# Record slots in two arrays, blockwise normalizations and a shorter node stage in a four-layer graph network

## The chip, the cores and the metric

The kernel runs on one core of a Trainium2 chip. The metric is the device time of one execution in microseconds (us). Engines are named as in the profile: PE (matrix products), PEld (its weight loads), DVE (vector), ACT (scalar), POOL (GpSimd) and SP (which here issues transfers). "L359" is line 359 of the kernel before.

## The reference

A graph of 6,250 nodes with 64 features each and 206,250 directed edges (each of 100,000 drawn edges in both directions, and a loop at each node), with 64 features and one of four types per edge. Each layer normalizes the nodes and adds its result to them:

```python
h = relu(layernorm(x)); x = x + L0(h)   # attention: softmax over each node's incoming edges
h = relu(layernorm(x)); x = x + L1(h)   # degree-normalized graph convolution
h = relu(layernorm(x)); x = x + L2(h)   # messages, below
h = relu(layernorm(x)); x = x + L3(h)   # gated graph network: 4 steps, a sum per edge type, then a GRU cell

def L0(h):
    qk, v = h @ qk_w.T + qk_b, h @ v_w.T + v_b
    s = clip(sum(qk[dst] * qk[src]) / 8, -5, 5)
    out = segment_sum(softmax_over(dst, s) * v[src], dst) @ o_w.T + o_b
    return layernorm(out + h) * ln_g + ln_b

def L2(h):
    f = relu([h[src], h[dst], edge] @ W1_f + b1_f) @ W2_f + b2_f    # summed at dst
    r = relu([h[dst], h[src], edge] @ W1_r + b1_r) @ W2_r + b2_r    # summed at src
    agg = segment_sum(f, dst) + segment_sum(r, src)
    return h + relu([agg, h] @ Wn1 + bn1) @ Wn2 + bn2
```

## The kernel before

Nodes stand in NB = 49 blocks of P = 128, and the blocks of destinations in NG = 7 groups of GB = 7. W = 7 x 128 = 896.

**Sort.** The kernel first sorts the edges by pairs of blocks (destination, source). Each edge gets a record of RW = 70 floats (six small fields and its 64 features) and a slot in a DRAM array, `rec_d`. The array has 7 x 50 = 350 tiles (NC = 50: one for each source block, and one more, the overflow of the pair of a block with itself, whose edges include the loops). A tile has 896 slots: 128 ranks for each of 7 destination blocks, rank first. Slots that no edge takes must hold an empty record (-1 in the first four fields, then zeros), so ACT's queue first fills the array: seven transfers (L215) with 128 rows of 25 packets of 3,920 bytes each, all from one small SBUF tile, `fill`.

Meanwhile DVE derives everything that the sort needs of the keys, in instructions over all EC = 1,620 columns (the edges as 128 x 1,620): block numbers `bd` and `bs`, six fields `cf`, the pair's `key`, the slot's `base` (L221 to L251). The keys go transposed to DRAM (`row_d`, L244). The first normalization follows, then a loop over 162 groups of G = 10 columns (`order`, written out by hand for PE, ACT, DVE and SP). In each group:

- `load`: SP loads the transposed keys (`kr`, and `br` on 49 partitions) and the edge features (`rec`), two groups ahead.
- `count` (L270 to L296): one-hot tables of the blocks on DVE, their running counts on PE (`pc`), written by ACT as `y`.
- `room_of`: the counts for this group's edges, on PE (`pr`).
- `settle` (L330 to L357): DVE works out each edge's rank among those of its pair and the slot `pos`. Ranks run as negative numbers; a chain of eleven small 128x10 instructions (L339 to L356) ends in `pos`, then L357 copies the fields into `rec`, and POOL scatters ten times 128 records (L359).
- Beside it, layer 0's projections (`projected`) in the first groups, then its edge weights: one block of scores on PE (L402), clipped on DVE (L408), exponentiated on ACT (L409).

Edges that find no room in their tile go to slots behind the array and through lists; these inputs have none.

**Dense build.** For each of the 350 tiles, the records (`r`, 128 partitions of 1,960 bytes) are loaded, one-hot matrices made and multiplied, which gives block matrices `ak_d` of edge counts and the attention's sums. At the end of each group, `places` writes node places to DRAM (L630): 128, 128 and 94 rows of 256-byte pieces.

**Layer 0's end and layers 1 to 3.** Layer 0's output (`project`, `store_o`), its normalization and additions run over all 49 blocks in single instructions; so do the normalizations ahead of the other layers (`normalize`, L119 to L131, and `pre_norm`, L135). Layer 1 multiplies with the block matrices. Layer 2 makes tables of two products of h per block (`tables`; the tile `tk`, one buffer, filled by ACT L178 and DVE L179, written by POOL L1006), then goes through the 350 tiles: messages in `ph` on PE (L1054), `m` by ACT and DVE (four buffers), sums at destinations (`accf_d` in DRAM) and at sources (`acc_r`). The node stage loads the first sum whole (`acc_f`) and runs 13 iterations of four blocks: 16 transposes (L1172), the second layers of both messages (`pg`, L1176 to L1178), the two products of the node network's first layer (`pz`, L1182 and L1183) and its second layer (`po`, L1188). Layer 3 multiplies with the block matrices four times (L813).

Of the kernel before, what the change touches and what calls it, by code (L numbers as in the profile page):

```python
# [19 lines left out]
P = 128  # L20
# [6 lines left out]
class Plan:  # L27
# [7 lines left out]

    def __init__(self, n_nodes, n_edges, gb=7, group=10):
        self.N, self.E = n_nodes, n_edges
        nb = -(-n_nodes // P)
        self.NG = -(-nb // gb)
        self.GB = -(-nb // self.NG)  # L40
        self.NB = self.NG * self.GB
        self.NC = self.NB + 1
        self.NP = self.NB * P
        self.W = self.GB * P
        self.NSLOT = self.NG * self.NC * self.W
        self.G = group
        self.EC = -(-n_edges // (P * group)) * group
        self.EP = self.EC * P
        assert self.NB <= P and self.NB * self.NB <= 4094
        assert self.NSLOT + self.EP < 1 << 24 and K * self.NP < 1 << 24  # L50
        assert self.G * self.NB <= 512 and 512 < self.W <= 1024 or self.NG == 1
# [3 lines left out]
def gnn_stack(ctx: ExitStack, tc: tile.TileContext, pl: Plan, a: dict, out: bass.AP):  # L55
# [42 lines left out]
    nc.sync.dma_start(x, a["x"].rearrange("(b p) d -> p b d", p=P))  # L98
# [3 lines left out]
    rec_d = dram.tile([pl.NSLOT + pl.EP, RW], F32, name="rec_d")  # L102
    rec_v = rec_d[: pl.NSLOT, :].rearrange("(t p j) r -> t p j r", p=P, j=GB)
# [10 lines left out]


    def normalize(dst, src_t, pool):

        s = pool.tile([P, NB], F32, name="ln_s")
        nc.vector.tensor_reduce(s, src_t, axis=AX.X, op=OP.add)  # L119
        m = pool.tile([P, NB], F32, name="ln_m")  # L120
        nc.vector.tensor_scalar(m, s, 1.0 / D, None, op0=OP.mult)
        nc.vector.tensor_tensor(dst, src_t, m[:, :, None].to_broadcast([P, NB, D]), op=OP.subtract)
        sq = pool.tile([P, NB, D], F32, name="ln_sq", bufs=1)
        nc.vector.tensor_tensor(sq, dst, dst, op=OP.mult)
        v = pool.tile([P, NB], F32, name="ln_v")
        nc.vector.tensor_reduce(v, sq, axis=AX.X, op=OP.add)
        sd = pool.tile([P, NB], F32, name="ln_sd")
        nc.scalar.activation(sd, v, AF.Sqrt, bias=eps, scale=1.0 / D)
        r = pool.tile([P, NB], F32, name="ln_r")
        nc.vector.reciprocal(r, sd)  # L130
        nc.vector.tensor_tensor(dst, dst, r[:, :, None].to_broadcast([P, NB, D]), op=OP.mult)  # L131

    def pre_norm(pool):
        normalize(h, x, pool)
        nc.vector.tensor_scalar(h, h, 0.0, None, op0=OP.max)  # L135
# [46 lines left out]
    with ExitStack() as st:  # L182
# [3 lines left out]


        cf = sp.tile([P, EC, RF], F16, name="cf")
        nc.vector.memset(cf[:, :, 4], 1.0)
# [10 lines left out]
        nc.vector.tensor_scalar(minus, ident[:NB, :NB], -1.0, None, op0=OP.mult)  # L200

        with tc.tile_pool(name="prep", bufs=1) as pp:
            keys = {}
            for n in ("dst", "src", "ety"):
                keys[n] = pp.tile([P, EC], I32, name="k_" + n)
                nc.sync.dma_start(keys[n], a[n])

            many = max(f for f in (1, 2) if NC % f == 0)
            fill = sp.tile([P, many * GB, RW], F32, name="fill")
            nc.vector.memset(fill, 0.0)  # L210
            nc.vector.memset(fill[:, :, 0:4], -1.0)
            fill_v = rec_d[: pl.NSLOT, :].rearrange("(p i j) r -> p i (j r)", p=P, j=many * GB)
            per = NC // many
            for i in range(NG):
                nc.scalar.dma_start(fill_v[:, i * per : (i + 1) * per, :],  # L215
                                    fill.rearrange("p j r -> p (j r)")[:, None, :]
                                    .to_broadcast([P, per, many * GB * RW]))
            ti = pp.tile([P, EC], I32, name="ti")
            bf = pp.tile([P, EC], F32, name="bf")
            for n, b in (("dst", bd), ("src", bs)):  # L220
                nc.vector.tensor_scalar(ti, keys[n], 7, None, op0=OP.arith_shift_right)  # L221
                nc.vector.tensor_copy(b, ti)
            nc.vector.tensor_copy(bf, bd)
            for f, n in ((0, "dst"), (1, "src")):
                nc.vector.tensor_scalar(ti, keys[n], P - 1, None, op0=OP.bitwise_and)
                nc.vector.tensor_copy(cf[:, :, f], ti)
            for f, m, s in ((3, P - 1, 1), (5, 1, 0)):
                nc.vector.tensor_scalar(ti, keys["dst"], m, s, op0=OP.bitwise_and, op1=OP.arith_shift_right)
                nc.vector.tensor_copy(cf[:, :, f], ti)
            nc.vector.scalar_tensor_tensor(cf[:, :, 2], keys["ety"], float(P // 2), cf[:, :, 3],  # L230
                                           op0=OP.mult, op1=OP.add)
            nc.vector.tensor_scalar(cf[:, :, 5], cf[:, :, 5], 255.0, 1.0, op0=OP.mult, op1=OP.add)
            nc.vector.scalar_tensor_tensor(key, bd, float(NB), bs, op0=OP.mult, op1=OP.add)
            nc.vector.tensor_scalar(key, key, -float(NB * NB // 2), None, op0=OP.add)

            with tc.tile_pool(name="rowps", bufs=2, space=PSUM) as ps:
                for c0 in range(0, EC, P):
                    n = min(P, EC - c0)
                    pt = ps.tile([P, 2, P], F32, name="pt")
                    nc.tensor.transpose(pt[:n, 0, :], key[:, c0 : c0 + n], ident)  # L240
                    nc.tensor.transpose(pt[:n, 1, :], bf[:, c0 : c0 + n], ident)
                    rt = pp.tile([P, 2, P], F16, name="rt", bufs=3)
                    nc.vector.tensor_copy(rt[:n], pt[:n])
                    nc.sync.dma_start(row_d[:, c0 : c0 + n, :].rearrange("k t e -> t k e"), rt[:n])  # L244

            grp = pp.tile([P, EC], F32, name="grp")
            nc.vector.tensor_scalar(grp, bd, float(GB), None, op0=OP.is_ge)
            for k in range(2, NG):
                nc.vector.scalar_tensor_tensor(grp, bd, float(k * GB), grp, op0=OP.is_ge, op1=OP.add)
            nc.vector.scalar_tensor_tensor(base, bs, float(W), bd, op0=OP.mult, op1=OP.add)  # L250
            nc.vector.scalar_tensor_tensor(base, grp, float(NC * W - GB), base, op0=OP.mult, op1=OP.add)  # L251
# [10 lines left out]
        with tc.tile_pool(name="l0i", bufs=1) as wk:  # L262
            pre_norm(wk)

        sw = s2.enter_context(tc.tile_pool(name="sortw", bufs=3))
        ps = s2.enter_context(tc.tile_pool(name="sortps", bufs=2, space=PSUM))

# [34 lines left out]
        nc.gpsimd.iota(aside, pattern=[[1, G]], base=pl.NSLOT, channel_multiplier=EC,  # L302
# [22 lines left out]
        def settle(i, kr, rec, pr):  # L325
# [15 lines left out]
            nc.vector.scalar_tensor_tensor(pf, r, -float(GB), base[:, gs], op0=OP.mult, op1=OP.add)  # L341

            t1 = sw.tile([P, G], F32, name="t1")
            nc.vector.tensor_scalar(t1, bs[:, gs], -float(W), float((NB - 1) * W), op0=OP.mult, op1=OP.add)
            nc.vector.scalar_tensor_tensor(t1, r, -float(P), t1, op0=OP.is_le, op1=OP.mult)
            nc.vector.tensor_tensor(pf, pf, t1, op=OP.add)

            room = sw.tile([P, G], F32, name="room")
            nc.vector.tensor_tensor(room, bd[:, gs], bs[:, gs], op=OP.is_equal)
            nc.vector.tensor_scalar(room, room, -float(P - 1), -float(P), op0=OP.mult, op1=OP.add)  # L350
            ov = over[:, gs]
            nc.vector.tensor_tensor(ov, r, room, op=OP.is_le)
# [5 lines left out]
            for t in range(G):  # L358
                s = nc.gpsimd.indirect_dma_start(  # L359
                    out=rec_d, out_offset=bass.IndirectOffsetOnAxis(ap=pos[:, t : t + 1], axis=0),  # L360
                    in_=rec[:, t, :], in_offset=None)
                tc.declare_no_dep(s.ins, group="records", reason="each edge has its own slot")
                tc.add_to_no_dep_group("records", s.ins)

        def projected():

            for k, n0 in enumerate(range(0, pl.NP, 512)):
                n = min(512, pl.NP - n0)
                s = slice(n0, n0 + n)
                b0, nb = n0 // P, n // P  # L370
                hT = hTs[k % 2]
# [40 lines left out]
        def order():  # L412
            groups = EC // G
            ahead = [load(k) for k in range(min(2, groups))]
# [26 lines left out]
            for i in range(groups):  # L441
                share = scored(i)
# [90 lines left out]
    with ExitStack() as st:  # L533
# [11 lines left out]
        def load(g, c):  # L545
            r = wk.tile([P, GB, RW], F32, name="r", bufs=4)
            nc.sync.dma_start(r, rec_v[g * NC + c])
# [188 lines left out]
    with l0 as st:  # L736
# [45 lines left out]

        project(ot, wox, store_o, ps)
        nc.vector.tensor_tensor(h, h, bo[:, None, :].to_broadcast([P, NB, D]), op=OP.add)
        y = ve[:, :, :D]
        normalize(y, h, wk)
# [632 lines left out]
```

## Time and profile before

| | us |
| --- | --- |
| median of 10 runs | 10,071.1 (10,043.1 to 10,078.5) |
| profiled execution, its own time | 10,060.0 |
| its span in the profile | 10,058.3 |
| start: fill, preparation of the keys, first normalization | 0 to 252 (first scatter 252.57) |
| sort loop | to 2,746 |
| dense build | 2,746 to 4,190 |
| end of layer 0, normalization | 4,198 to 4,294 |
| layer 1 and layer 2's start | to 4,554 |
| messages | 4,554 to 7,304 |
| node stage | 7,304 to 7,417 |
| normalization ahead of layer 3 | 7,417 to 7,445 |
| layer 3 | to the end |

The boundaries are read from the timeline. In the page's second part each digit is the busy share of an engine in one of 40 slices of the span, 251 us each. In the groups' part, "busy, mean ns | idle before" says how long instructions of one kind took and how long their engine had nothing to do ahead of them, with what ended that idle time.

### The profile page before, as it was taken

What the parts mean: (1) busy time and instruction counts of PE and PEld (TensorE: products, weight loads), DVE (VectorE), ACT (ScalarE), POOL (GpSimd) and SP (SyncE); (2) the same over time, 40 slices, a digit from 0 to 9 for tenths busy, and PEclk for the clock granted to TensorE, in tenths of its full rate; (3) what the DMA queues carried; (4) which work ended last, traced back from release to release, by engine and by line L of the source; (5) the groups of instructions that cost most, each with busy time, mean ns of one, the idle gap of its engine ahead of it and who ended that gap; (6) DMA issues with size and microseconds to landing.
All of it is one profiled execution on the core that took longest, in us unless ns stands there. A gap on an engine that the chain in (4) does not pass through costs nothing. (4 is left out here: it accounts for less than half of the span.)

```text
span 10058.3 us, 146718 instructions
## 1 busy us (share of the span) xinstructions
PE 8128.2 (81%) x47524; PEld 6476.5 (64%) x47524; DVE 7495.4 (75%) x17172; ACT 5684.3 (57%) x8738; POOL 2905.5 (29%) x3651
## 2 busy tenths in 40 slices
PE   1444444444499999778999999999989999999999
PEld 0222222222244444367999999999958888888888
DVE  3566666666699999875677777777748888788788
ACT  0111111111166665455677777777748888888887
POOL 0666666666633333202222222222210000000000
PEclk9555565555599999878999999999989999999999
DMA  9444444444488887654544444444428878788777
GB/s 377 125 142 146 147 150 143 144 149 149 143 280 284 285 283 268 207 163 162 153 139 136 146 139 137 146 139 137 130 94 261 257 241 262 230 261 264 231 258 241
DMA packets 1035148, 1948.57 MB, mean 194 GB/s; under 512 B 327021, under 2 KB 579668, under 8 KB 1034214
## 3 DMA queue, kind: packets, MB, share of 16 engines
q1 hardware_dynamic: 748436, 1287.54, 41.3%
q10 hardware_dynamic: 224658, 564.27, 16.7%
q0 software_dynamic: 61248, 87.08, 2.6%
q8 instruction: 377, 6.18, 0.3%
q14 instruction: 429, 3.51, 0.1%
HBM read 1433.65 MB, written 504.81 MB: 193 GB/s over the span
## 5 line engine op out<-in xcount | busy, mean ns | idle before, releaser
L813 PE MATMUL ph<-mr,t 128*128 128x512 f32 x10976 | 2315.7, 370 | 12.4 <-DVE mr L799 9.0
L799 DVE CAST mr<-m 128x896 fp32r<-128x896 uint8 x3293 | 1951.0, 624 | 355.8 <-PE ph L813 239.6
L813 PEld LDWEIGHTS ph<-mr,t 128*128 128x128 f32 x10976 | 1987.9, 188 | 275.6 <-DVE mr L799 16.3
L797 ACT CAST mr<-m 128x896 fp32r<-128x896 uint8 x2195 | 1963.5, 940 | 311.7 <-PE ph L813 238.2
L359 POOL DMA_INDIRECT rec_d<-rec,pos x1620 | 1611.2, 995 | 1133.8 <-issue 448.7
L1062 DVE SCALAR_TENSOR_TENSOR m<-ph,m 128x512 fp32r<-128x512 f32 x1400 | 871.7, 623 | 424.1 <-ACT m L1061 392.4
L1078 POOL TENSOR_TENSOR acc_r<-acc_r,prc 128x128 f32<-128x128 f32 x784 | 611.1, 779 | 1801.9 <-ACT prc L1076 1771.2
L1061 ACT ACTIVATE m<-ph 128x512 fp32r<-128x512 f32 x1400 | 762.7, 545 | 571.7 <-PE ph L1054 530.8
L293 PE MATMUL pc<-os,od 128*49 128x441 bf16 (+4 forms) x1619 | 396.3, 409 | 813.4 <-DVE os L270 650.0
L1054 PE MATMUL ph<-pc,st 128*128 128x256 f32 x4802 | 1009.0, 291 | 0.0
L1054 PE MATMUL ph<-qb,dt 128*128 128x256 f32 x4900 | 990.2, 284 | 0.0
L1054 PE MATMUL ph<-wc,eat 128*128 128x256 f32 x4900 | 989.8, 284 | 0.0
L599 ACT CAST ak<-pa 128x512 uint16<-128x512 f32 x1372 | 696.0, 533 | 388.2 <-PE pa L593 334.1
L293 PEld LDWEIGHTS <-od 128*49 128x49 bf16 x1619 | 228.5, 147 | 1034.9 <-DVE od L270 483.4
L409 ACT ACTIVATE e<-e 128x896 f32<-128x896 f32 x343 | 324.3, 945 | 926.0 <-DVE e L408 509.8
L1054 PEld LDWEIGHTS ph<-qb,dt 128*128 128x128 f32 x4900 | 762.5, 191 | 0.0
L1054 PEld LDWEIGHTS ph<-wc,eat 128*128 128x128 f32 x4900 | 759.4, 190 | 0.0
L1054 PEld LDWEIGHTS ph<-pc,st 128*128 128x128 f32 x4802 | 747.6, 192 | 8.1 <-DVE m L1062 6.6
L593 PE MATMUL pa<-kd,s 128*128 128x256 f16 x2401 | 687.9, 287 | 21.6 <-DVE kd L575 21.6
L296 ACT ACTIVATE y<-pc 49x490 f16<-49x490 f32 x162 | 92.8, 573 | 1068.7 <-remote 693.7
L402 PE MATMUL pst<-qs,kt 128*128 128x512 f32 x1372 | 574.4, 563 | 124.6 <-DVE e L408 60.5
L336 DVE SCALAR_TENSOR_TENSOR eq<-kr,key,earlier 128x128 f16<-128x128 f16 x1620 | 475.3, 347 | 265.0 <-DVE eq L336 142.3
(277 smaller groups left out, 14240.4 us busy)
## 6 DMA issues: line engine op xcount, KB each, us to landing
m<-ak_d SPq DMA_DIRECT2D x1372, 448.0 KB
r<-rec_d SPq DMA_DIRECT2D x700, 245.0 KB
e_d<-e ACTq DMA_DIRECT2D x343, 448.0 KB
e<-e_d SPq DMA_DIRECT2D x343, 448.0 KB
ak_d<-ak ACTq DMA_DIRECT2D x343, 448.0 KB
pc<-p_d SPq DMA_DIRECT2D x343, 256.0 KB
rec_d<-fill ACTq DMA_DIRECT2D x7, 12250.0 KB
rowst<-lid_d ACTq DMA_DIRECT2D x350, 224.0 KB
```

The lines of the kernel that those rows point to most:

```text
L293: nc.tensor.matmul(pc[:, t:, :], l_, r_.to_broadcast([r_.shape[0], G - t, NB]), start=k == 0, stop=k == len(terms) - 1, skip_group_check=True)
L359: s = nc.gpsimd.indirect_dma_start(out=rec_d, out_offset=bass.IndirectOffsetOnAxis(ap=pos[:, t : t + 1], axis=0), in_=rec[:, t, :], in_off ...
L402: nc.tensor.matmul(pt[:, o : o + n], kt[:, c * P : (c + 1) * P], qs[:, k, o : o + n], start=k == 0, stop=k == 1)
L593: nc.tensor.matmul(pa, l_[:, j, :], r_[:, j, :], start=j % 2 == 0 and n == 0, stop=n + 1 == len(pairs), skip_group_check=True)
L599: nc.scalar.copy(ak2[:, :, (j + 1 - n) * HP : (j + 1) * HP].rearrange("p k (n q) -> p n k q", n=n), pa2[:, :n])
L797: nc.scalar.copy(m, src_t)
L799: nc.vector.tensor_copy(m, src_t)
L813: nc.tensor.matmul(ph[:, o : o + n], parts(c, k), r[:, o : o + n], start=(c == 0 and k == 0), stop=(c == NB - 1 and k == kk - 1))
L1054: nc.tensor.matmul(o, l_, r_, start=(q == 0 and j == j0), stop=(q == 5), skip_group_check=True)
L1061: nc.scalar.activation(mh, ph4, AF.Relu)
L1062: nc.vector.scalar_tensor_tensor(ml, ph4, 0.0, mh.bitcast(F32), op0=OP.max, op1=OP.subtract)
L1078: nc.gpsimd.tensor_tensor(acc_r[:, cb, :], acc_r[:, cb, :], prc[:, k * MSG : (k + 1) * MSG], op=OP.add)
```

## The change

Slots. There are now two arrays behind each other in `rec_d` (after the places for edges without room, so that `base` gets EP added). The first 32 ranks of a tile live in the first array, ranks 32 to 127 and the overflow tiles in the second. The first array is filled by `fill_first`, three transfers ahead of everything; the second by `fill_others`, thirteen transfers, one of them issued in each of the first thirteen groups. Both take the tiles as rows: 128, 128 and 94 of 350, in 16 packets a row for the first array, 12 a row in each of four quarters for the second, and one transfer of 7 rows for the overflow tiles. Edges of the first LEAD = 16 groups go to the first array alone (a rank of 32 or more would have no room there; there is none), so their scatters wait for `fill_first` alone. Later groups choose the array by rank, with two more small instructions. Two transfers load a tile's records in place of one.

Preparation. Keys are loaded and prepared in chunks of 120 columns (`prepare`), each nine groups ahead of its use, inside the loop; the first normalization goes by seven blocks (`first_norm`) between the first groups' projections.

Normalizations elsewhere go by seven blocks too (`normalize` is a generator), the maximum with zero is joined with the last product, and what follows (layer 0's additions, layer 1's products and splits) is done block by block. Layer 2's normalization is woven with the making of its tables, `tk` has two buffers, `m` three.

Node stage. The second layers of the messages are multiplied once with the first half of Wn1 (`wm`), the biases of the messages go with the lower half (`wd`). Each iteration then has three transposed inputs in place of four and three products in place of five, and loads its part of the first sum itself.

```diff
+    rec_d = dram.tile([pl.EP + 2 * pl.NSLOT, RW], F32, name="rec_d")
+    rec_p = [rec_d[pl.EP + k * pl.NSLOT : pl.EP + (k + 1) * pl.NSLOT, :] for k in range(2)]
+    rec_f = [r.rearrange("(t s) r -> t (s r)", s=W) for r in rec_p]
...
+    def load_records(r, t, ci):
+        if ci == NB:
+            nc.sync.dma_start(r, rec_v[1][t])
+        else:
+            nc.sync.dma_start(r[:R0], rec_v[0][t][:R0])
+            nc.sync.dma_start(r[R0:], rec_v[1][t][R0:])
...
+        def fill_up(to, f):
+            n = to.shape[0]
+            to = to.rearrange("t (i e) -> t i e", e=many * GB * RW)
+            f.dma_start(to, fill[:n, None, :].to_broadcast(list(to.shape)))
+        def fill_first():
+            for t0 in range(0, NT, P):
+                fill_up(rec_f[0][t0 : min(NT, t0 + P), : R0 * GB * RW], nc.scalar)
+        def fill_others():
+            step = (P - R0) // 4 * GB * RW
+            for t0 in range(0, NT, P):
+                for q in range(4):
+                    o = R0 * GB * RW + q * step
+                    fill_up(rec_f[1][t0 : min(NT, t0 + P), o : o + step], nc.scalar)
+                    yield
+            fill_up(rec_p[1].rearrange("(g t s) r -> g t (s r)", t=NC, s=W)[:, NB, : R0 * GB * RW], nc.scalar)
...
-            for i in range(NG):
-                nc.scalar.dma_start(fill_v[:, i * per : (i + 1) * per, :],
-                                    fill.rearrange("p j r -> p (j r)")[:, None, :]
-                                    .to_broadcast([P, per, many * GB * RW]))
...
+            if i < pl.LEAD:
+                nc.vector.tensor_scalar(ov, r, -float(R0), None, op0=OP.is_le)
+            else:
...
+                nc.vector.tensor_scalar(t1, r, -float(R0), float(pl.NSLOT), op0=OP.is_le, op1=OP.mult)
+                nc.vector.tensor_tensor(pf, pf, t1, op=OP.add)
...
             for i in range(groups):
+                k, at = divmod(i, CH // G)
+                if k + 1 < len(chunks):
+                    if at == 1:
+                        keys.append(load_keys(k + 1))
+                    elif at == 3:
+                        prepare(k + 1, keys.pop())
+                next(others, None)
...
+        nc.vector.tensor_tensor(h, h, bo[:, None, :].to_broadcast([P, NB, D]), op=OP.add)
         project(ot, wox, store_o, ps)
-        nc.vector.tensor_tensor(h, h, bo[:, None, :].to_broadcast([P, NB, D]), op=OP.add)
...
+        for b in normalize(y, h, wk):
...
-            msgs = [bp.tile([P, 2, 2, MR], F32R, name=f"m{k}") for k in range(4)]
+            msgs = [bp.tile([P, 2, 2, MR], F32R, name=f"m{k}") for k in range(3)]
...
-                        t = wk.tile([P, 2, 2, 2 * MSG], F32R, name="tk", bufs=1)
+                        t = wk.tile([P, 2, 2, 2 * MSG], F32R, name="tk")
...
-            for name, t, m in (("f", acc_f, MSG), ("r", acc_r, MSG), ("d", deg2, 2), ("h", h, D)):
+            for t, m in ((acc_r[:, b0 : b0 + n], MSG), (hd, D + 2), (af, MSG)):
...
+            for k, (l_, r_) in enumerate(zip((wm[1], wd, wm[0]), ts)):
+                nc.tensor.matmul(pz[:, :w], l_, r_[:, :w], start=k == 0, stop=k == 2)
```

`prepare(k)` issues 28 DVE instructions on 120 columns: the block numbers, the key, four fields cut from the keys and cast, two more fields and a constant, the group number and the slot's base; and on PE two transposes, whose copy `rt` SP writes to `row_d`.

## The prediction

> **What bounds the kernel now.** The sum is made against the profiled execution, whose span is 10,058.3 us and whose own time is 10,060.0 us, 11 us under the median of the runs shown (10,071.1); a difference under 0.2% (20 us) can't be told from no change.
>
> I read the page first. VectorE (DVE) is the only engine near full in slices 8 to 16, GpSimd (POOL) has its work only up to slice 11, and the first slice is filled by DMA alone.
>
> ```profile
> span 10058.3 us, 146718 instructions
> ...
> DVE  3566666666699999875677777777748888788788
> ...
> POOL 0666666666633333202222222222210000000000
> ...
> GB/s 377 125 142 146 147 150 143 144 149 149 143 280 284 285 283 268 207 163 162 153 139 136 146 139 137 146 139 137 130 94 261 257 241 262 230 261 264 231 258 241
> ```
>
> The timeline of the start shows what ACT does there: seven fills of 12,250 KB, each 128 rows, and then the square root that they kept waiting.
>
> ```profile
> 7.62 191.82 ACTq L215 DMA_DIRECT2D rec_d<-fill  x7
> 199.63 1.28 ACT L128 ACT_TABLE_LOAD   x1 [199.63 <-issue]
> ```
>
> ACT comes free at 199.4, but the DMA summary of 205 to 252 us still counts 3,713 fill packets, 232 on each of 16 engines; with 5.6 us more at the pace below, some 267 an engine are queued when ACT is let go. Alone, the fills run at 392 GB/s: 16 x 3,920 bytes in 0.160 us, so 0.160 us for a packet on one engine (in the packet times, 0.153 to 0.171). The first scatter starts at 252.57, the record copy of group 2 ends the fill's phase at 281.7, and that of group 12 (L357) starts at 440.1.
>
> Then the sort loop runs to 2746. The waits of 300 to 2600 say who sets its pace: POOL scatters for 12.7 us a group and waits for DVE.
>
> ```profile
> POOL rec_d L359 <- issue: 414.2, 1351, 2.0
> POOL rec_d L359 <- DVE rec L357: 394.6, 114, 11.7
> ```
>
> The copies of L357 stand 15.36 us apart. DVE's own row of the same stretch, 1,477 us busy of 2,300, is 9.9 us of work a group; the rest is short idle time between its instructions:
>
> ```profile
> L339 DVE SCALAR_TENSOR_TENSOR rank<-rank,wi 128x10 f32<-128x10 f32 x149 | 25.7, 172 | 97.1 <-remote 75.6 <-DVE eq L336 17.6
> L345 DVE SCALAR_TENSOR_TENSOR t<-rank,t 128x10 f32<-128x10 f32 x149 | 25.5, 171 | 35.4 <-DVE t L344 25.3 <-issue 3.6 <-remote 3.2
> L346 DVE TENSOR_TENSOR pf<-pf,t 128x10 f32<-128x10 f32 x149 | 25.4, 170 | 26.1 <-DVE t L345 20.5 <-issue 2.0
> ```
>
> So work added to DVE in a group shows in full, unless it lies in one of its waits.
>
> **The fills, the largest term.** Records now go to two arrays, filled by transfers whose first dimension is the tile: 128, 128 and 94 tiles of 350. What a 94-row transfer does is in the trace already: L630 writes 128 rows (64 KB) twice and then 94 rows (47 KB) in each group. The DMA summaries of two windows around 4196.5 and 4199.7, where little else moves:
>
> ```profile
> GB/s 0 23 114 137 91 114 182 182 250 137 205 273 228 319 159 250 296 250 250 205 228 250 206 183 159 182 159 182 137 114 91 114 46 68 23 0 23 0 0 0
> ...
> q1 hardware_dynamic: 272, 0.07, 67.3%
> ```
>
> ```profile
> DMA  0011911111111111111111111111119911111110
> GB/s 0 14 22 43 498 36 36 36 43 29 43 29 43 29 43 29 43 29 43 29 43 29 43 29 43 29 43 29 43 29 274 490 43 29 43 29 43 29 43 7
> ...
> q1 hardware_dynamic: 190, 0.05, 15.1%
> ```
>
> The first is 2 x 128 packets and 16 closing ones, done within 0.4 us; the second 2 x 94 and 2 closing ones, spread over 1.4 us at a tenth of the engines (the two high slices are instruction fetches). 188 packets took 1.35 us, 0.0144 us each on two engines; 94 rows ran on two engines of 16. [...]
>
> Engine 0 then carries, in fill packets: fill_first 128 + 128 + 94 x 16 / 2 = 1,008; the eight 128-row pieces 8 x 96 = 768; four 94-row pieces 4 x 94 x 12 / 2 = 2,256; the last 7-row piece 16. That is 4,048 instead of 1,400, and 648 us at 0.160. Beside them run the loads and scatters of 13 groups: the shares of the two queues in 300 to 2600 (24.1% and 7.4%) make 4.8 us of an engine a group, 63 us; the start's other loads cost 8 (the first three slices of the first 205 us move 83, 226 and 359 GB/s). ACT, which issues one piece a group in front of the next group's y (L296), is let go of the twelfth piece when 267 packets (43 us) are left: 7.6 + 648 + 8 + 63 - 43 = 684, and group 12's copy follows some 8 us later, at 692 instead of 440: **+250**. Groups 13 to 15 need only the first array, and group 16's scatter comes 60 us later, when the last piece has landed. Ends: 0.153 us and 2.3 us a group (14.8% of 47 us for three groups, as in 205 to 252) give 632, +190; 0.171 us gives 733, +290. Everything that prepares chunks 0 and 1 and the first normalization is hidden in this phase; without it that cover is gone (10 us a chunk).
>
> **prepare.** Twelve further chunks are prepared inside the loop by 28 DVE instructions each, work that lay under the fill. The whole-width instructions (L189 to L251 without L243) sum to 48 us; a chunk is 120 of 1,620 columns: 3.6 us. A fixed part per instruction comes on top: 28 x 0.17 us (the 128x10 rows' busy time) is 4.8, 28 x 0.305 (their mean pitch, waits included) 8.5. So 8.3 to 13.5 us with the wait for two transposes; I take 10, nearer the low end since many of the 28 are independent: **+120** (100 to 162). [...] The row_d write (SP) stands in front of the next loads and waits for the copy rt; loads run two groups ahead (30 us), which covers it.
>
> **settle.** 146 groups get two more dependent 128x10 instructions (compare with 32 slots, add). Eleven such take 3.36 us a group, 0.305 each: 0.61 x 146 = **+89**. Pairs of them range from 0.29 to 0.88 us: +42 to +128. The 16 first groups lose five, inside the fill.
>
> **Dense build.** Each block's record load becomes two (32 and 96 rows, both multiples of 16). DMA is at 83% there, DVE and PE at 96%: nothing, some 5 us if SP's second issue (0.36 us) shows.
>
> **Normalizations and node stage.** L0 to L1 (4198 to 4294): fourteen whole-width DVE instructions of 3.42 us are cut in seven and woven with the seven 3.0 us output blocks; DVE keeps its work, so -8 (-20 to +5). L1 to L2: the last add (3.42), the 5.29 memset and about half of the 26 us of normalization go under the table steps, -21 (-35 to 0). The tables: tk has two buffers instead of one. In 4554 to 4910 PE waits
>
> ```profile
> ACT tk L178 <- DMA p_d<-tk: 37.3, 11, 4.5
> PE pe L946 <- DVE tk L179: 36.3, 11, 4.1
> ```
>
> which is the same 37 us seen twice: -37 (-60 to -15). Next late there is the POOL queue that writes the tables. The three message buffers wait for nothing new, since PE has issued the scatter of the oldest before the matmul that the next write waits for. Node stage: 11 us from the load of acc_f to the first transpose, mostly gone (-8); 13 iterations of 7.72 us lose 4 transposes (0.5), and two matmul pairs (0.98 and 1.05), so 13 x 2.5 = 33, less new waits: -25 (-35 to -15). L3's start: 22.7 us of normalization and 1.8 of maximum go between the node stage's matmuls, the 5.29 memset stays: -20 (-25 to -10). Together **-120** (-150 to -80).
>
> Sum: 250 + 120 + 89 - 120 = +339, 10,399, say 10,400. All low ends: +182; all high ends: +500.
>
> **Rivals.** (A) Faster: the 94-row fills use all 16 engines. Then 1,400 packets an engine remain, ACT is let go of the first array's issues by about 40 us, groups run at the 21.4 us apiece that the trace shows under the fill, and group 12 comes at about 310, -130: -130 + 120 + 89 - 120 = -41, 10,019. For it speaks only that ACT's queue shows no 94-row transfer; with four engines (2,544 packets, +9) the whole is still slower, from eight on (1,792 packets, -111) it is faster. (B) DVE's 5.3 us of idle time a group swallow most of its new work: 209 becomes 60, and the time 10,250. Against it: much of that idle time is between dependent instructions, which an addition doesn't fill. (C) The loads of the first groups, on the same two engines, alternate with fill packets one by one and ACT waits for both: another 100 us, 10,500.
>
> **How the numbers follow.** Forecast 0.72, A 0.07, B 0.12, C 0.09. The range 10,245 to 10,510 takes in B and C and the bounds but not A. Faster: most of A, 0.06. Same: the rest of A and a third of a slip in B, 0.03. Slower: 0.91.
>
> **What would show it.** Right: ACT's 94-row issues of 90 to 105 us each; two closing packets; POOL idle from the ninth to the twelfth group; group 12's copy at 630 to 730; a loop pitch of 15.9 to 16.2 us, 10 us more in each twelfth group; 7304 to 7445's counterpart shorter by some 50 us. Wrong: fill pieces of the 94 rows that end as fast as the 128-row ones, or a group 12 before 450.

## The result and the profile after

The changed kernel takes 10,260.8 us (median of 8 runs, 10,246.6 to 10,270.3) against 10,067.7 (28 runs): 1.0195 of the time before, 95% interval 1.0186 to 1.0204, 193 us slower. The profiled execution of the changed kernel took 10,290.3 us, 30 more than its median; that of the kernel before 10,060.0, 8 less than its own. So the two profiles stand 230 us apart, 37 more than the medians.

From the page of the changed kernel, the rows shown of the kernel before:

```profile
span 10288.5 us, 149366 instructions
...
DVE  2226666666668999998777777777758878888787
...
POOL 1226666656663433330322222222220000000000
...
GB/s 215 173 87 142 143 147 142 136 137 148 141 137 254 282 284 284 274 222 182 192 144 145 137 138 145 138 137 143 135 93 264 260 227 262 241 252 262 229 262 241
```

The first three slices (257 us each) now move 215, 173 and 87 GB/s, where the first alone moved 377, and DVE and POOL are busy for only one to two tenths of them. The waits of POOL from 185 to 740 us say for what: its first scatter waits for the first array's fill, twelve later ones for DVE's record copy (the numbers are us in total, times, the longest).

```profile
POOL rec_d L436 <- DVE rec L434: 378.7, 12, 83.1
POOL rec_d L436 <- DMA rec_d<-fill: 183.9, 1, 183.9
```

ACT's timeline has the reason behind DVE (each row has the start and how long the issue held ACT). The first 94-row piece of `fill_others` is issued at 330.9 within 0.3 us; each of the four issues behind it (three more such pieces and the seven-row one) holds ACT for 76 to 88 us, and the next group's `y` stands behind each. The first three of these issues end 12 to 14 us ahead of the closing packets of the piece ahead (428.7, 520.3 and 613.2 against 440 to 442, 533 to 534 and 625 to 627).

```profile
330.87 0.27 ACTq L220 DMA_DIRECT2D rec_d<-fill  x1
...
352.76 75.89 ACTq L220 DMA_DIRECT2D rec_d<-fill  x1
...
433.16 87.16 ACTq L220 DMA_DIRECT2D rec_d<-fill  x1
...
529.07 84.15 ACTq L220 DMA_DIRECT2D rec_d<-fill  x1
...
617.72 88.27 ACTq L220 DMA_DIRECT2D rec_d<-fill  x1
```

What a 94-row piece makes of the DMA engines stands in the summary of 100 to 165 us, where the third piece of `fill_first` runs alone: one tenth of the engines, 51 GB/s where the fills before ran at 392. With the two closing packets that such a piece has, this is two engines with a packet of 3,920 bytes every 0.154 us each, an estimate from the 51.

```profile
DMA  1111111111111111111111111111111111111117
GB/s 51 51 51 51 51 51 51 51 51 48 51 51 51 51 51 51 51 51 51 51 51 51 48 51 51 51 51 51 51 51 51 51 51 51 51 51 51 48 51 275
```

By stage, from the two traces. The last column is the difference of two traces taken later, where the kernel before takes 9,699 to 9,709 us. The record numbers the chips of these later runs 1, 3 and 15 and gives no number for the first profiles, so it does not show whether those come from another chip; "the first chip" stands for theirs, "the other chip" for any of the three. The two traces of the last column are from chip 3. All experiments below ran on these three, each beside runs of the kernel before, so ratios are taken there and not across.

| us | forecast | before | after | difference | difference on the other chip |
| --- | --- | --- | --- | --- | --- |
| start of group 12's record copy | +250 | 440.1 | 713.9 | +274 | +293 |
| from there to the last scatter | +209 | 2,305.5 | 2,398.6 | +93 | -5 |
| dense build | 0 | 1,444.2 | 1,448.0 | +4 | 0 |
| end of layer 0 | -8 | 101.8 | 92.6 | -9 | -9 |
| layer 1's sums | 0 | 143.4 | 148.8 | +5 | +6 |
| to the first message | -21 | 115.8 | 83.9 | -32 | -22 |
| messages | -37 | 2,752.4 | 2,692.8 | -60 | -61 |
| node stage | -33 | 113.7 | 70.9 | -43 | -43 |
| ahead of layer 3 | -20 | 40.3 | 26.4 | -14 | -14 |
| layer 3 | 0 | 2,601.1 | 2,612.4 | +11 | -5 |
| whole span | +339 | 10,058.3 | 10,288.5 | +230 | +141 |

A few us in a stage say nothing: in the eight profiles of kernels with the old tables, the stage up to the first message took 107 to 116 us and the messages 2,747 to 2,757; layer 3, the same in all fourteen, took 2,594 to 2,617.

### The profile page after: what moved, and what is told of

It is laid out like the page before. It is cut to its first block, busy times and chain, and to the rows that moved or that the text cites. A ratio compares the mean times of both kernels' runs of the same rounds, so it can differ in the third digit from the quotient of the medians.

```text
span 10288.5 us, 149366 instructions
## 1 busy us (share of the span) xinstructions
PE 8099.6 (79%) x47434; PEld 6463.9 (63%) x47434; DVE 7583.0 (74%) x17991; ACT 5683.5 (55%) x8756; POOL 2949.3 (29%) x3651
## 5 line engine op out<-in xcount | busy, mean ns | idle before, releaser
L1187 PE MATMUL pr<-m,so 128*128 128x260 f32 x2450 | 651.8, 285 | 22.3 <-ACT prc L1192 22.3
```

The lines of the kernel that those rows point to most:

```text
L1187: nc.tensor.matmul(pr, v["so"][:, j, :], m[:, j - j0, 1, :], start=(c is None or j == 0), stop=(c is None or j == GB - 1))
```

## The experiments

**1. The fills' rows.** The 94-row pieces are cut in two, nothing else changes.

```diff
-            for t0 in range(0, NT, P):
-                fill_up(rec_f[0][t0 : min(NT, t0 + P), : R0 * GB * RW], nc.scalar)
+            for rows in [[(0, 128)], [(128, 256)], [(256, 336), (336, 350)]]:
+                for t0, t1 in rows:
+                    fill_up(rec_f[0][t0:t1, : R0 * GB * RW], nc.scalar)
```

and likewise in `fill_others`, where both pieces of a quarter are issued in the same group.

> The changed kernel, with its 94-row fills cut into 80 and 14 rows (80 is a multiple of 16; 14 has 14 as its divisor). The theory (94 rows run on two engines): engine 0 then carries about 1,400 fill packets as in the kernel before, ACT is let go of the first array's issues by 40 to 60 us, group 12's record copy comes at 300 to 330 us instead of 714, and the time falls by 380 to 410 us to 9,850 to 9,880, under the kernel before. The rival (the fills are late because ACT issues sixteen of them, in order, between the groups' work, whatever engines carry them): four more issues of the same kind, so group 12 stays near 700 us and the time within 40 us of 10,261.

Measured: 9,496.6 us against 9,698.8, ratio 0.9793 (0.9779 to 0.9806), 202 us faster than the kernel before. Group 12's copy starts at 366.4, 345 us sooner than the unchanged change on that chip (711.8, below), and later than the 300 to 330 expected: ACT is let go of the first array's issues at 60.6, the late end of the 40 to 60 expected, and from group 0's copy (82.1) to group 12's a group takes 23.7 us while loads and fills share the engines, where 21.4 was assumed. The time falls by 349 us against the changed kernel's 9,845.8 there, where 380 to 410 was expected. There are five more issues from the same queue, and group 12 does not stay near 700, so the rival falls. The same window of the DMA summary, 100 to 165 us:

```profile
DMA  9999999899999999999999999999999999877799
GB/s 291 408 364 364 392 413 353 335 394 379 382 389 384 339 383 415 379 366 360 380 397 397 375 379 392 376 407 411 409 421 389 293 302 352 332 269 272 216 260 264
```

**2. Is it the divisor?** The same edit with 88 and 6 rows, neither a multiple of 16.

> The changed kernel with the 94 rows cut into 88 and 6, both no multiples of 16. If the engine count is the largest number up to 16 that divides the rows, these transfers close with 11 and 6 packets, engine 0 carries some 1,500 to 1,550 fill packets and group 12 comes 15 to 40 us later than with 80 and 14 (366 us). If only multiples of 16 are spread well (rival), the 88 rows are as slow as the 94 and group 12 stays at 700.

Measured: group 12's copy at 400.7, 34 us later than with 80 and 14; one run, 9,533.3. On ACT's queue a transfer closes with packets of 4 bytes: 16 for the 128 rows that ran at 392 GB/s in the kernel before, 2 for the 94 rows at 51 GB/s, so their number is taken for that of the engines. Counted in the traces from 25 us to the last fill, they are 112 before (seven fills of 16), 177 in the changed kernel (32 + 2, 8 x 16, 4 x 2, and 7 for the seven-row piece), 317 with 80 and 14 and 252 with 88 and 6. The last two sums are met to the last packet by 16 and 14, and by 11 and 6, as the expectation has it for 88 and 6. By an estimate with these numbers of engines, engine 0 has 1,616 fill packets here (400 + 768 + 432 + 16; the expectation's 1,500 to 1,550 was added up wrongly) and 1,424 with 80 and 14 (352 + 768 + 288 + 16): 192 x 0.160 = 31 us, beside the 34 measured. So a count of rows that is no multiple of 16 wasn't bad in itself: for all seven counts that ran here (128, 94, 88, 80, 14, 7 and 6 rows, on ACT's queue and with a broadcast source) the closing packets add up with each count's largest divisor up to 16.

**3. The keys prepared in the first groups.** On top of experiment 1:

```diff
...
-                k, at = divmod(i, CH // G)
-                if k + 1 < len(chunks):
-                    if at == 1:
-                        keys.append(load_keys(k + 1))
-                    elif at == 3:
-                        prepare(k + 1, keys.pop())
+                if i + 2 < len(chunks):
+                    keys.append(load_keys(i + 2))
+                if i + 1 < len(chunks):
+                    prepare(i + 1, keys.pop(0))
```

> The same, and chunk k+1 of the keys is prepared in group k (k = 0 to 12) in place of one chunk in each twelfth group, so that all of it lies in the phase in which fills and loads set the pace. If prepare costs what the two profiles show in the loop (8 us a chunk, 90 to 100 us in all) and DVE has that time idle in the first groups: 80 to 100 us less than with the cut fills alone. If DVE is as late in those groups as later (rival): the first thirteen groups grow by the same 8 us each and nothing is gained, within 20 us.

Measured: 9,522.9 us, ratio 0.9821 (0.9807 to 0.9834): 26 us more than without it, so the 80 to 100 us were not there. Group 12's copy starts at 393.7 instead of 366.4, and from there to the last scatter it is 1,965.5 us against 1,964.1. The rival's first half did not hold either: the first groups grew by 1.9 us each and not by 8. Nothing could be gained because in the later loop the chunks cost nothing on that chip, as experiments 4 to 6 show.

**4. settle's two instructions alone**, in the kernel before (the compare's result is multiplied by 0, so the slots stay the same):

```diff
+            nc.vector.tensor_scalar(t1, r, -32.0, 0.0, op0=OP.is_le, op1=OP.mult)
+            nc.vector.tensor_tensor(pf, pf, t1, op=OP.add)
```

> The kernel before, with one more dependent pair of 128x10 DVE instructions in settle in every group (a compare whose result is multiplied by 0, and an addition). The prediction's step (added DVE work shows in full, 0.305 us an instruction): 2 x 0.305 x 162 = 99 us more, 10,167. Its rival B (DVE's idle time of 5.3 us a group takes it up, as the pitch of 15.35 us in the changed kernel's ordinary groups suggests): within 20 us of before.

Measured: 9,697.4 against 9,698.8, ratio 0.9998 (0.9989 to 1.0007). With three such pairs:

> The same with three such pairs in every group. In full: 6 x 0.305 x 162 = 296 us more. If the idle time takes it up: under 60 us more. If only a part of it is free, the slope from the first pair to the three tells it: each pair beyond what is free costs up to 99 us.

Measured: 9,717.8, ratio 1.0021 (1.0012 to 1.0030), +19 us of the 296. Of these 14 lie ahead of group 12's copy (432.7 against 418.4 without the pairs); from there to the last scatter it is 1,971.6 against 1,971.2. It was run once more, in case it should meet the slower loop:

> The kernel before with three more pairs in settle, once more. Where the loop runs at 12.7 us a group, +20 us again. Where it runs at 15.4: up to +296 if DVE sets that pace, under +60 if something else does.

Measured: 9,709.6 beside 9,709.4, one run. The copies again came 12.6 us apart, and group 12 at 433.6, so the slower loop's answer is not there.

The additions are not free for DVE, though. Here are the 13 record copies of groups 12 to 24 without a pair, with one and with three (the last two numbers ahead of the semicolon are the first and the last start):

```profile
L357 DVE CAST rec<-cf x13: 193/194/360, 418.4 to 537.8; 128x60 f32<-128x60 f16 x13
```

```profile
L359 DVE CAST rec<-cf x13: 193/194/323, 423.5 to 549.7; 128x60 f32<-128x60 f16 x13
```

```profile
L363 DVE CAST rec<-cf x13: 193/196/355, 432.7 to 568.8; 128x60 f32<-128x60 f16 x13
```

That is 9.95, 10.52 and 11.34 us a group: 0.57 for one pair, where the prediction has 0.61, and 1.39 for three. The time does not show it because another engine is later, as experiments 5 and 6 say.

**5. Both kernels unchanged, for their traces there.**

> The kernel before, unchanged, for its trace on the chip of this call. In the call before, runs of the kernel before took 9,699 us, and a loop with a pair of instructions added showed a pitch of 12.6 us a group with POOL never idle, where the first profile shows 15.36 with POOL waiting for DVE. If the chip or its moment sets which of the two holds, this trace has one of the two pitches and nothing between, and all stages after the sort loop stay within 5 us of the first profile's. If the added pair was what speeded the loop up (rival), the pitch here is 15.4.

Measured: 9,709.4 us. The copies stand 12.71 us apart on average, without any added pair, and POOL does not wait for DVE any more (waits of 500 to 1900 us):

```profile
POOL rec_d L359 <- issue: 291.5, 956, 0.3
POOL rec_d L359 <- DMA rec_d<-rec,pos: 19.5, 64, 0.3
POOL rec_d L359 <- DVE e L408: 4.9, 16, 0.3
```

POOL's own pace is 13.14 us from a group's first scatter to the next group's (ten at 1.31 on average, 1.27 in the median). DVE's copies run ahead of it: group 12's by 1 us, group 48's by 87, the last by 90, and from group 50 to 150 they come at POOL's 13.1. So 12.71 is the mean of a faster start and POOL's pace. The stages behind the sort loop are within 3 us of the first profile's (layer 3: 6.5); of the 351 us between the two profiles of this kernel, 334 lie between group 12's copy and the last scatter and 22 ahead of it.

> The changed kernel, unchanged, beside before on the same chip. Where the loop runs at POOL's 12.7 us a group, the last 94-row fill still lands at about 750 us and the sort ends 162 - 13 groups later: group 12 at 700 to 720 instead of 424, +285, and prepare and settle cost nothing (POOL covers them), -147 behind the sort: about +140, a ratio of 1.014. Where the loop runs at 15.4: the ratio of 1.0195 again. If DVE's additions show in both cases (the prediction's sum): +240 or more, 1.024.

Measured: 9,845.8 against 9,700.8, ratio 1.0150 (1.0133 to 1.0167), +145 us. That is the first case: +293 until group 12, nothing for prepare and settle, -143 from the dense build to layer 3's start, and layer 3's -5.

**6. Half of POOL's scatters**, in the kernel before; every second column's records are never written:

```diff
-            for t in range(G):
+            for t in range(0, G, 2):
                 s = nc.gpsimd.indirect_dma_start(
```

> The kernel before with every second scatter left out (half of the records are never written). If DVE sets the loop's pace, as the prediction has it, the pitch stays where before_again has it, within 0.4 us. If POOL's ten scatters of 1.27 us set it, or slow DVE's own instructions, the pitch falls to what DVE needs without them, 10 to 12 us.

Measured: the pitch of the copies falls from 12.71 to 10.19 (9,254.6 us), and now it is POOL that waits (500 to 1900 us):

```profile
POOL rec_d L359 <- DVE rec L357: 534.5, 135, 6.8
```

There POOL sets the pace of the full kernel, 13.1 us, and DVE with its 10.2 has some 2.9 us a group to spare.

> The kernel before with every second scatter left out (half of the records are never written), once more: on the chip of the first time the pitch fell from 12.7 to 10.2 us. Where the loop runs as in the first profile (15.4 us a group) it stays there, if DVE's own short waits make it, and falls to 10 to 11 if they come from POOL's scatters. Where it runs at 12.7, 10.2 again.

Measured: 10.17 us a group, 9,256.2 us; again no slower loop was met.

**7. The table's second buffer alone**, in the kernel before, with three buffers for m:

```diff
-                        t = wk.tile([P, 2, 2, 2 * MSG], F32R, name="tk", bufs=1)
+                        t = wk.tile([P, 2, 2, 2 * MSG], F32R, name="tk")
```

> The kernel before with two buffers for tk in place of one, and three for m in place of four (the space). The two profiles show the messages at 2,752 us before and 2,693 after, -60 where -37 was forecast, and -32 ahead of them. If the second buffer of tk does all of the first: -60 from the messages and some -10 from the eight table steps ahead of them, 0.6 to 0.7%. If it is only the 37 us in which PE waited for it: -37 to -45. If PE or POOL is late next (nothing gained): within 10 us.

Measured: 9,609.1 against 9,709.4, ratio 0.9895 (0.9880 to 0.9911), 100 us (86 to 117). The messages take 2,676.0 us where the kernels with the old tables take 2,747 to 2,757, and the stage ahead of them 99.3 in place of 107 to 116. The rows of tk, first without (experiment 5's kernel before) and then with the second buffer ("first to last start"), show the stretch in which tables are made beside messages: 336.6 us and 272.9.

```profile
L178 ACT CAST tk<-pe x42: 372/586/590, 4202.7 to 4539.3; 128x512 fp32r<-128x512 f32 x40, 128x256 fp32r<-128x256 f32 x2
```

```profile
L178 ACT CAST tk<-pe x42: 360/587/589, 4183.6 to 4456.5; 128x512 fp32r<-128x512 f32 x40, 128x256 fp32r<-128x256 f32 x2
```

The stretch without the second buffer varies: 328 to 338 us in the eight profiles. So 55 to 65 of the 71 to 81 us gained in the messages are the tables', where PE's waits for tk made 37.

**8. The node stage alone**, in the kernel before, with its products of weights made ahead of the messages.

> The kernel before with the shorter node stage alone (with its products of weights made ahead of the messages). The prediction's step: -25 and -8, 33 in all; the changed kernel's trace: 113.7 to 70.9, -43. If the stage is worth by itself what the trace shows: -40 to -45, less up to 5 for the weights' products. If a part of it came from the normalization that follows in the changed kernel (rival): -30 to -35.

Measured: 9,654.1 against 9,709.4, ratio 0.9946 (0.9933 to 0.9960), 52 us (39 to 65). Its stage takes 70.3 us in place of 113.0, all of the changed kernel's 43; the rest of the 52 is in stages that it does not touch (layer 3: 2,593.6 against 2,607.6; the messages 7 and the stage ahead of them 6 less) and within their scatter between runs.

## Why the prediction was right, and where not

**Right: the fills.** The step from the 47 KB write's two closing packets to two engines, and from 4,048 packets on engine 0 to ACT's queue, gave 692 us for group 12's copy. That ACT's queue would spread 94 rows over two engines, and the seven rows of the last piece over seven (its 16 packets an engine), was the author's assumption, which no run of the kernel before shows; the changed kernel's trace has two closing packets for 94 rows, at 51 GB/s, and nine for the last such piece and the seven-row one together. The copy came at 713.9, with POOL idle from the ninth to the twelfth group. The fill itself was sized well: its last packet starts at 721.5, where the working gave 684 + 43 = 727. Three of its four 94-row issues in the loop held ACT for 76 to 87 us (the first for 0.3), where 90 to 105 each was named as a sign: ACT does other work for 4 to 9 us before the next, and the issues end 92 to 93 us apart (428.7, 520.3, 613.2, 706.0), 564 packets an engine at 0.16. What was not sized well is the release of ACT: it is let go some 16 us before the fill's end and not 43, because group 12's copy also stands behind the seven-row piece's issue (the copy of group 11 at 623.9 and that of group 12 at 713.9 follow the issues that end at 613.2 and 706.0). Cutting the rows takes the whole term away and leaves a gain, which shows its cause (on the other chip; the cut rows did not run on the first).

**Wrong: "work added to DVE in a group shows in full".** This carried +89 for settle and +120 for prepare; 93 of the 209 appeared on the first chip and none on the other. The first reading behind it, DVE near full in slices 8 to 16, is not in the row shown: DVE has six tenths up to slice 11, where the loop ends, and the nines belong to the dense build, where PE has them too (99999 in slices 12 to 16 of its row). The second, that POOL waits for DVE and so DVE's work sets the pace, left rival B's 5.3 us a group of idle time within DVE's own stream aside with an argument: an addition does not fill idle time between dependent instructions. In the changed kernel's first profile the groups without a chunk stand 15.35 us apart, with two more instructions, against 15.36. Their pair is there (0.42 us from L423's start to the next instruction's), but L408's ten (L336 before) lost as much idle time (842 to 3080 us):

```profile
L408 DVE SCALAR_TENSOR_TENSOR eq<-kr,key,earlier 128x128 f16<-128x128 f16 x1400 | 406.4, 347 | 164.9 <-DVE eq L408 99.1 <-remote 55.3 <-issue 10.4
L423 DVE TENSOR_SCALAR t<-rank 128x10 f32<-128x10 f32 x140 | 25.9, 185 | 12.5 <-DVE pf L422 8.0
L424 DVE TENSOR_TENSOR pf<-pf,t 128x10 f32<-128x10 f32 x140 | 24.4, 175 | 19.6 <-DVE t L423 14.0 <-issue 1.3
```

164.9 us in 140 groups is 1.18 a group; the kernel before had 265.0 in the page's 162 groups, 1.64 (its row stands in the last section for 500 to 1900 us: 1.75). So settle was rival B, and its term is 0 in place of 89. That the pair was taken up by just this idle time is read from the two rows and was not tried. The sign named for the loop, a pitch of 15.9 to 16.2, looks right by chance: the mean is 16.01, but of 15.35 in ordinary groups, for which the sum had 15.97, and 23.5 in those with a chunk.

**prepare** has the right mechanism on the first chip and the wrong size: the twelve groups with a chunk took 23.5 us on average, 8.2 more than the others, 98 in all where 120 was forecast from 10 us a chunk. Why was not separated. On the other chip the copies of such groups come 18.7 us after the one before, but the other groups stand 12.0 apart and POOL's backlog covers it: POOL starts a group every 13.07 us.

**Mis-sized: the stages behind the loop**, -148 up to layer 3 where -120 was summed. The table's term took only PE's 37 us of wait for tk; the stretch with tables shortened by 55 to 65 with the second buffer alone, and the steps ahead of it by 8 to 16 (experiment 7). The changed kernel's stretch with tables is as short (273.4 us), but its messages take 2,692.8 us against 2,676.0 there; what takes those 17 (two loads for each record tile, the normalization's use of a buffer) was not separated. Of the 32 gained up to the first message, forecast as 21, some 10 lie within that stage's scatter. The node stage gave 43 for 33: from its first to its last output it went from 86.8 to 56.7 us (a full iteration from 7.72 to 5.01), 30 of the 33 that PE's removed instructions come to (25 were taken), and its start, from the last sum to the first output, from 26.8 to 14.2 (8 forecast). Ahead of layer 3, 14 for 20.

**The number.** 10,261 lies 16 us above the lower end of the range, 11 from rival B's 10,250 and 139 from the forecast's 10,400. In the profiles +230 stands for the sum's +339: the start 24 dearer, the loop 116 cheaper, the stages up to layer 3 28 cheaper, layer 3 itself 11 dearer and within its scatter. So the range holds the result because it took in B, and the direction is owed to the fills' term; the sum itself had the loop wrong. On the other chip the same change cost 145 us.

**Rivals.** A is refuted by the closing packets (2 for 94 rows, 16 for 128); C, which asked for another 100 us, by group 12's copy, 22 us behind the forecast. B held on the first chip for settle and not for prepare. On the other chip both cost no time, but not by B's mechanism: DVE's copies do come later, by 0.57 us for settle's pair where 0.61 was priced (experiment 4), and POOL's pace covers it.

**Open.** Why the first chip's loop has a pitch of 15.36: its DVE is idle for 159.4 us ahead of L336 in 500 to 1900 us, where on the other chip it is for 0.0 (last section). In the twelve profiles of the experiments that slower loop was not met again, so whether POOL's scatters cause it there, and what else would have absorbed settle's pair, was not tried in it.

## What to carry to other kernels

Before rows of a transfer are chosen, look in the trace for a transfer with that row count and count its closing packets: a remainder of 94 rows, with 2 closing packets and 51 GB/s where 128 rows had 16 and 392, cost more than anything else in this change (without it group 12's copy came 345 us sooner), and cutting it into 80 and 14 made the version that beats both kernels (0.9793 of the time before, on the other chip). That one engine waits for another does not say that work added to the other shows in full: here a pair cost nothing where POOL waited for DVE (15.35 us a group with it and 15.36 without), and nothing where it did not (ratio 0.9998). Test that with one dummy pair before pricing added work, and read the pace from the engine that ends last: the copies' mean of 12.7 us hid a lead of up to 90 us over scatters at 13.1. And the wait shown at one engine is not the whole of what a second buffer gives: here it was 37 of 55 to 65 us.

## What the runs showed of the hardware that was not expected

The same kernel's sort loop ran at 15.4 us a group in the first profile and at 13.1 in one taken later, on chip 3 (POOL's first scatters; its copies 12.7 apart), with the same instructions; layer 3 and the messages differed by under 0.3%. Much of the difference shows as idle time of DVE ahead of L336, 1.75 us a group against 0.0; of its 159.4 us the trace puts 85.3 down to DVE's own earlier instructions. On the first chip, from 500 to 1900 us:

```profile
L336 DVE SCALAR_TENSOR_TENSOR eq<-kr,key,earlier 128x128 f16<-128x128 f16 x910 | 267.5, 347 | 159.4 <-DVE eq L336 85.3 <-remote 56.0 <-issue 17.4
```

and on the other:

```profile
L336 DVE SCALAR_TENSOR_TENSOR eq<-kr,key,earlier 128x128 f16<-128x128 f16 x1110 | 310.9, 349 | 0.0
```

Each instruction takes as long as before (347 and 349 ns); the 159 us between them are gone, and 1,110 are done in place of 910 in the same 1,400 us. On the first chip POOL is in a scatter in 63% of these 159 us and in 65% of the whole 1,400, so the idle time does not go with POOL's scatters at that moment; what causes it stays open.
